# One PSUM tile for the attentions of a restoration block: scores in a ring of seven banks, and half of the keys' 3x3 on VectorE

## The chip, the cores and the metric

The kernel runs on one core of one Trainium2 chip. The metric is the device time of one execution in microseconds. Before the change it is 4100.66 us, the median of three runs (4098.43 to 4103.39). The core has five engines with queues of their own: TensorE (PE, matmuls; PEld are its weight loads), VectorE (DVE), ScalarE (ACT), GpSimd (POOL) and SyncE (SP, which issues the transfers). Matmul results land in PSUM, which has 128 partitions of eight banks, each of 512 float32 values.

## The reference, cut to what matters

The network has four layers, each `x + layer(group_norm(x))`, on an input of 2 images, 128 channels, 64x64 pixels, in float32. Only layer 0 is touched. For each image:

```python
xn = biasfree_ln(gn(x), ln1_w)                    # over the channels
qkv = conv1x1(xn, w_qkv)                          # 128 -> 640 channels
qkv = depthwise_3x3(qkv, w_dw)                    # 640 groups
q1, k1, v, q2, k2 = split(qkv, 5)                 # 128 channels each, 4 heads of 32
q1, k1, q2, k2 = l2 norms over the 4096 tokens of each channel
attn1 = softmax(q1 @ k1.T * temperature)          # 4096 x 4096 per head
out1 = attn1 @ v
attn2 = softmax(q2.T @ k2 * temperature)          # 32 x 32 per head
out = conv1x1(out1 + v @ attn2, w_po)
x = x + conv1x1(biasfree_ln(out, ln2_w), w_proj) + b_proj
```

## The kernel before, in words

Layer 0 is `_layer0`. It goes through the two images in turn: norm, convolutions, attention, finish. The norm of image 1 runs as side work inside the attention of image 0, and the finish of image 0 inside the convolutions of image 1.

**Convolutions** (`convolutions`). The five groups of 128 channels are numbered q1 0, k1 1, v 2, q2 3, k2 4, and each is computed in two halves of 32 image rows, written (group, half). A half first goes through the 1x1 (`pointwise`, L1556): 33 rows (32 and one for the border) in chunks of 16, 16 and 1 rows, into pairs of banks and one single bank, from which ScalarE copies them into a zero-padded frame (L1563). Then comes the 3x3. For q1, k1, q2, k2 it is on TensorE (`depthwise`, L1578): nine taps, each as 16 matmuls of 32x32 diagonal blocks with 512 columns, into two pairs of banks. The banks come out with rows and columns of the head blocks interchanged, and for q1 and k1 eight copies on ScalarE and eight on VectorE (`in_place`, L1598) put the pieces where they belong. For v the 3x3 is on VectorE (`value_taps`, L1614 and L1616): nine operations on 128x2048. Next the squares of each channel are summed (L1603), q1 is scaled by both norms, v is transposed into `vt` (`value_tiles`), and q2 and k2 are transposed and multiplied into one 128x512 accumulator (`products`). All of this is in `_in_order`: each engine keeps the order of the program. The frame for a 3x3 is made two 3x3 ahead.

**Attention** (`attention` with `_attn_four`). There are eight blocks of 512 queries (qb) and 32 tiles of 128 keys (kt), so 256 steps per image. A step computes the scores of the four heads: for each head, whose 32 channels are one row group of TensorE, two matmuls with 64 keys each (L1373), into two pairs of banks. Two Exps of 128x1024 follow on ScalarE (L1382) into a tile `weights` (four buffers). One step later four matmuls (L1790) multiply the weights by `vt` into one accumulator bank. The softmax's denominators: VectorE adds the weights of eight steps (seven adds of 128x2048, L1830) and four matmuls with ones (L1790 too) add that sum to a second accumulator bank. After four such groups, in the fourth step of the next query block, VectorE transposes that bank (L1803), takes the reciprocal, transposes back and multiplies. The order of the instructions here is chosen by a scheduler when the kernel is built; TensorE's is scores of step n+1, then values of step n.

**PSUM.** There are three pairs of banks, `sp()`, taken in turn by the scores, the 1x1, the 3x3 and all side work, and two single banks, `acc(0)` and `acc(1)`.

## Time and profile before

The profiled execution took 4107.57 us; its span from the first to the last instruction is 4105.7 us. Busy times by stage, in us (the span's time, then each engine):

| stage | span | PE | DVE | ACT |
|---|---|---|---|---|
| norm of image 0 | 0 to 37 | 14.7 | 26.6 | 15.8 |
| convolutions, image 0 | 37 to 180 | 131.3 | 74.2 | 64.4 |
| attention, image 0 | 180 to 790 | 599.8 | 541.3 | 513.4 |
| finish of 0 and convolutions, image 1 | 790 to 990 | 176.3 | 113.6 | 77.8 |
| attention, image 1 | 990 to 1590 | 593.5 | 539.2 | 504.5 |
| finish of image 1 | 1590 to 1640 | 38.5 | 38.0 | 6.9 |

The other layers follow until 4105.7. A group's line shows the line of the kernel, the engine, the operation, out<-in with the shapes, the count, busy time and mean ns of one, and the idle time just before with what ended it. The chain of waits lists, in order of time, start, length and what was running or awaited. A timeline gives start, length, engine, line and operation of consecutive instructions, and in brackets the idle time before with its releaser. A float32 matmul leaves two records. Their ends are modelled, so TensorE's busy time includes short waits inside a block.

### The profile page before, as it was taken

To read this page: it belongs to the slowest core of one execution; us is meant where nothing else is said; L and a number is where in the kernel's file an instruction comes from. 1 tells how busy PE (TensorE), PEld (TensorE's weight loads), DVE (VectorE), ACT (ScalarE), POOL (GpSimd) and SP (SyncE) were. 2 spreads that over 40 slices of the span, in tenths; PEclk is the share of its full clock that TensorE was granted. 3 is DMA by queue.
4 is the path that set the end of the run, shared out by engine and by line. 5 is a ranking of instruction groups with operands and counts; after the bars stand their busy time and mean duration, and the time that the engine had idled before them with its cause. 6 is when DMAs were issued, how large, how long until landed. Compare 5 with 4: busy or idle time off the path is not lost.

```text
span 4105.7 us, 83161 instructions
## 1 busy us (share of the span) xinstructions
PE 3941.3 (96%) x35790; PEld 1383.9 (34%) x35790; DVE 3182.5 (78%) x3526; ACT 3231.8 (79%) x3907; POOL 74.2 (2%) x145
## 2 busy tenths in 40 slices
PE   7999999989999998997898999999999999999998
PEld 4522222245222223445666233222322222222222
DVE  4689999846989998986775887777777777776666
ACT  4478888734888884334663899999999999999998
POOL 1001000000000001000000000000000000000000
PEclk9999999999999999998898999999999999999999
DMA  1199960000000000002662211020012101010000
GB/s 50 22 189 189 188 96 2 2 1 2 1 2 2 2 2 13 1 6 111 255 276 105 87 39 32 29 67 27 29 31 61 36 24 32 32 57 6 6 6 4
DMA packets 193134, 217.66 MB, mean 53 GB/s; under 512 B 30442, under 2 KB 154346, under 8 KB 188659
## 3 DMA queue, kind: packets, MB, share of 16 engines
q1 hardware_dynamic: 192754, 212.25, 19.9%
q8 instruction: 282, 4.62, 0.5%
q14 instruction: 98, 0.79, 0.1%
HBM read 178.64 MB, written 98.57 MB: 68 GB/s over the span
## 4 chain that ended last, share of the span: by engine, by line
PE 86%; DVE 8%; ACT 3%; issue 2%; POOL 0%; DMA 0%; SPq 0%; DVEq 0%; POOLq 0%; ACTq 0%
PE ps_acc L2193 24%; PE ps_s L2170 18%; PE ps_s L1373 13%; PE ps_acc L1790 12%; PE ps_sp L1578 4%; PE ps_bank L710 2%; DVE sums L1830 2%; PE ps_z L1008 2%; DVE e L950 1%; PE ps_t L640 1%; PE ps_sp L1556 1%; PE ps_bank L590 1%; PE ps_bank L1062 1%; PE ps_bank L681 1%; ACT weights L1382 1%
## 5 line engine op out<-in xcount | busy, mean ns | idle before, releaser
L2184 ACT ACTIVATE weights<-ps_s 128x1024 f32<-128x1024 f32 x1920 | 1781.8, 1063 | 75.9 <-PE ps_s L2170 75.8
L1382 ACT ACTIVATE weights<-ps_s 128x1024 f32<-128x1024 f32 x1024 | 993.8, 1024 | 168.8 <-PE ps_s L1373 151.1
L2193 PE MATMUL ps_acc<-weights,vt 128*32 128x512 f32 x8192 | 1093.9, 606 | 0.0
L1830 DVE TENSOR_TENSOR sums<-sums,weights 128x2048 f32<-128x2048 f32 x384 | 880.0, 2292 | 45.1 <-ACT weights L1382 8.2
L2170 PE MATMUL ps_s<-q,k 64*128 64x512 f32 x4096 | 830.5, 469 | 3.8 <-DMA k<-stack 2.7
L2170 PEld LDWEIGHTS ps_s<-q,k 64*128 64x128 f32 x4096 | 348.5, 184 | 936.5 <-ACT weights L2184 809.9
L1373 PE MATMUL ps_s<-q,k 32*64 32x512 f32 x8192 | 632.0, 614 | 3.4 <-ACT weights L1382 1.3
L1790 PE MATMUL ps_acc<-weights,vt 128*32 128x512 f32 x4096 | 550.0, 605 | 7.2 <-ACT used L1820 3.7
L2142 DVE SCALAR_TENSOR_TENSOR exp_z<-exp_z,exp_m 128x1024 f32<-128x1024 f32 x384 | 469.2, 1222 | 9.3
L2126 DVE TENSOR_SCALAR exp_i<-ps_s 128x1024 int32<-128x1024 f32 x128 | 156.8, 1225 | 216.8 <-PE ps_s L2170 216.6
L1373 PEld LDWEIGHTS ps_s<-q,k 32*64 32x64 f32 x8192 | 162.1, 130 | 434.8 <-PE ps_s L1373 337.0
L2193 PEld LDWEIGHTS ps_acc<-weights,vt 128*32 128x32 f32 x8192 | 161.9, 108 | 309.8 <-issue 309.0
L1790 PEld LDWEIGHTS ps_acc<-weights,vt 128*32 128x32 f32 x4096 | 81.2, 108 | 427.0 <-issue 403.5
L662 DVE SCALAR_TENSOR_TENSOR X<-g,w,X 128x2048 f32<-128x2048 f32 x84 | 197.4, 2351 | 2.6
L1830 DVE TENSOR_TENSOR sums<-weights 128x2048 f32<-128x2048 f32 x64 | 146.6, 2291 | 61.5 <-ACT weights L1382 61.1
L2146 DVE SCALAR_TENSOR_TENSOR weights<-exp_z,exp_i 128x1024 f32<-128x1024 f32 x128 | 156.8, 1225 | 15.2
L1578 PE MATMUL ps_sp<-pad,diag 32*32 32x512 f32 x4608 | 159.8, 600 | 2.3 <-ACT q L1598 1.3
L2142 DVE SCALAR_TENSOR_TENSOR exp_z<-exp_m 128x1024 f32<-128x1024 f32 x128 | 156.0, 1218 | 0.0
L1008 PE MATMUL ps_z<-w_ri,e 128*32 128x128 f32 x2048 | 137.3, 408 | 14.6 <-DVE e L950 12.3
L1578 PEld LDWEIGHTS ps_sp<-pad,diag 32*32 32x32 f32 x4608 | 96.0, 103 | 54.8 <-issue 17.7
L950 DVE TENSOR_SCALAR e<-ps_pe 32x136 f32<-32x136 f32 (+1 forms) x352 | 104.3, 296 | 4.9
L948 ACT ACTIVATE e<-ps_pe 32x136 f32<-32x136 f32 (+1 forms) x352 | 99.5, 283 | 4.1
(296 smaller groups left out, 2824.7 us busy)
## 6 DMA issues: line engine op xcount, KB each, us to landing
w_ri<-w_r SPq DMA_DIRECT2D x16, 2112.0 KB, 7.9
w_ri<-w_i SPq DMA_DIRECT2D x16, 2112.0 KB, 13.3
stack<-qs SPq DMA_DIRECT2D x64, 256.0 KB, 2.1
q<-stack SPq DMA_DIRECT2D x128, 128.0 KB, 2.5
k<-stack SPq DMA_DIRECT2D x128, 128.0 KB, 2.5
stack<-ks SPq DMA_DIRECT2D x32, 256.0 KB, 2.1
w_r<-in_L_conv_kr_w SPq DMA_DIRECT2D x15, 528.0 KB, 12.8
w_r<-in_L_conv_kr_x SPq DMA_DIRECT2D x15, 528.0 KB, 12.8
```

Of the source, the lines that this page charges most:

```text
L662: nc.vector.scalar_tensor_tensor(xi, g[:, i : i + H // 2, j : j + W], w8[:, s : s + 1], xi, ALU.mult, ALU.add)
L1008: nc.tensor.matmul(out.rearrange("p (n f o) -> p n f o", n=2, f=2), e[:, s, 2 * j : 2 * j + 2, :].rearrange("p f x -> p (f x)"), w.rearran ...
L1373: nc.tensor.matmul(ps[j // 2][to, j % 2, :], k[rows, kt * 128 + 64 * half : kt * 128 + 64 * half + 64], q[rows, qb * CH : (qb + 1) * CH], ...
L1382: nc.scalar.activation(w[:, 2 * p : 2 * p + 2, :], ps[p], AF.Exp)
L1578: nc.tensor.matmul(ps[r // 2][to, r % 2, :].rearrange("p (h w) -> p h w", w=W), diag[rows, grp, t, :], pad[rows, y0 : y0 + ROWS, t % 3 : t ...
L1790: nc.tensor.matmul(ac[n][rows, :], lhs(rows), w[:, j, :], start=first, stop=last)
L1830: nc.vector.tensor_add(parts[0].rearrange("p j c -> p (j c)"), t.rearrange("p j c -> p (j c)"), w.rearrange("p j c -> p (j c)"),)
L2126: nc.vector.tensor_scalar(i, ps.rearrange("p j c -> p (j c)"), EXP_SCALE, EXP_BIAS, ALU.mult, ALU.add)
L2142: nc.vector.scalar_tensor_tensor(z, x, n, m, ALU.add, ALU.mult)
L2170: nc.tensor.matmul(ps[j // 2][:, j % 2, :], g.k[kt // 4][rows, j // 2, keys], g.q[qb][rows, j // 2, :], start=True, stop=True,)
L2184: nc.scalar.activation(w[0], ps[p], AF.Exp)
L2193: nc.tensor.matmul(g.ac[32 * j : 32 * j + 32, :], g.vt[:, kt, j // 2, i : i + 2, :].rearrange("p a d -> p (a d)"), w[:, i, :], start=(at = ...
```

## The change

The change touches layer 0 alone.

- One PSUM tile `banks` of eight banks replaces the two pools. Outside the attention, `sp()` is a pair of its first six banks in turn and `acc(n)` is bank 6 or 7. Inside it, bank 7 is the accumulator of the values and banks 0 to 6 are a ring (`taken()`): a step takes the next four for its scores, and the sums and the side work (`half()`) take one each.
- A step has three Exps instead of two: one bank, two banks, one bank (or one, one, two where the ring wraps).
- The sums no longer have a bank of their own: twice per query block, two groups' sums are added in one bank of the ring by eight matmuls, and VectorE transposes it. The first time it keeps 16 columns (`first`), the second time it adds them and goes on as before. `sums` tiles have three buffers.
- The 3x3 of (1, 0), the first half of the keys, is done by VectorE's taps, as the values are; seven 3x3 on TensorE remain. The taps are spread over the iterations by a new table. The two halves of v are no longer made together: the second half's 1x1 comes two iterations later.
- `pointwise` takes its rows in chunks of 1, 8, 16 and 8, into `acc(0)`, `acc(1)`, a pair, and `acc(0)`.

```diff
+    psp = ctx.enter_context(tc.tile_pool(name="f0_ps", reuse_waits="tile", bufs=1, space=PSUM))
+    banks = psp.tile([128, 8, CH], F32, name="ps")
     def sp():
-        return spp.tile([128, 2, CH], F32, tag="sp", name="ps_sp")
+        n = at["pair"]
+        at["pair"] = (n + 1) % 3
+        return banks[:, 2 * n : 2 * n + 2, :]
     def acc(n):
-        return accp.tile([128, CH], F32, tag=f"acc{n}", name=f"ps_acc{n}")
+        return banks[:, 6 + n, :]
+    def taken():
+        n = at["bank"]
+        at["bank"] = (n + 1) % RING
+        return n
+    def half():
+        return banks[:, taken(), :] if attending[0] else sp()[:, 0, :]
...
-        for r0 in range(0, H // 2 + 1, 2 * ROWS):
-            n = min(2 * ROWS, H // 2 + 1 - r0)
-            ps = sp() if n > 1 else acc(0).rearrange("p (o c) -> p o c", o=1)
+        for r0, n in ((4 * ROWS, 1), (0, ROWS), (ROWS, 2 * ROWS), (3 * ROWS, ROWS)):
+            ps = sp() if n > ROWS else acc(int(r0 == 0)).rearrange("p (o c) -> p o c", o=1)
...
-        order = [(1, 0), (1, 1), (0, 0), (0, 1), (3, 0), (4, 0), (3, 1), (4, 1)]
+        order = [(1, 1), (0, 0), (0, 1), (3, 0), (4, 0), (3, 1), (4, 1)]
+        kpad = frame(pool, "vpad")
+        run(pointwise(kpad, 1, 0))
+        first = taps(1, 0, k1, kpad)
         frames = [frame(pool) for _ in range(2)]
-        for n in range(2):
-            run(pointwise(frames[n], *order[n]))
-        pads = [frame(pool, "vpad") for _ in range(2)]
-        taps = value_taps(pads)
+        run(pointwise(frames[0], *order[0]))
+        next(first)
+        run(pointwise(frames[1], *order[1]))
+        by_vector = first
...
             if n == 0:
-                for half in range(2):
-                    run(pointwise(pads[half], 2, half))
+                by_vector = chain(by_vector, values_of(0))
...
+            if n == 2:
+                squares_of(pool, k1, 0, ss[:, 1, :])
+                by_vector = chain(by_vector, values_of(1))
...
-            for _ in range((0, 0, 3, 3, 4, 4, 4, 0)[n]):
-                next(taps, None)
+            for _ in range(((5, 5, 5, 4, 4, 4, 0), (2, 6, 6, 4, 4, 4, 0))[b > 0][n]):
+                next(by_vector, None)
...
-            while pending:
-                qb, n, w = pending.pop(0)
-                if n == 0:
-                    ac[1] = acc(1)
-                four(1, lambda rows: ones, w, n == 0, n == len(SUMMED) - 1)
-                if n == len(SUMMED) - 1:
+            while len(pending) > 1:
+                (qb, n, one_part), (_, _, other) = pending.pop(0), pending.pop(0)
+                out = banks[:, taken(), :]
+                four(out, lambda rows: ones, one_part, True, False)
+                four(out, lambda rows: ones, other, False, True)
+                by_query = cp.tile([128, CH // 32, 32], F32, tag="g", name="by_query", bufs=1)
+                nc.vector.transpose(by_query.rearrange("p n i -> p (n i)"), out)
+                if n == 0:
+                    firsts[qb] = small.tile([128, CH // 32], F32, tag="first", name="first")
+                    nc.vector.tensor_copy(firsts[qb], by_query[:, :, 0])
+                    continue
...
+                rec = small.tile([128, CH // 32], F32, tag="rec", name="rec")
+                nc.vector.tensor_add(rec, by_query[:, :, 0], firsts.pop(qb))
+                nc.vector.reciprocal(rec, rec)
...
-            if i == 3:
+            if i == 3 and n % 2 == 0:
                 sums()
...
+        def steps():
+            waiting = []
+            for qb in range(NCH):
+                for kt in range(NQT):
+                    at_banks = [taken() for _ in range(4)]
+                    for j in range(4):
+                        rows = slice(32 * j, 32 * j + 32)
+                        for h in range(2):
+                            nc.tensor.matmul(
+                                banks[64 * h : 64 * h + 64, at_banks[j], :],
+                                k1[rows, kt * 128 + 64 * h : kt * 128 + 64 * h + 64],
+                                q1[rows, qb * CH : (qb + 1) * CH],
+                                start=True,
+                                stop=True,
+                            )
+                    w = pool.tile([128, 4, CH], F32, tag="weights", name="weights")
+                    pieces = ((0, 1), (1, 2), (3, 1))
+                    if at_banks[2] < at_banks[1]:
+                        pieces = ((0, 1), (1, 1), (2, 2))
+                    for j, n in pieces:
+                        first = at_banks[j]
+                        nc.scalar.activation(
+                            w[:, j : j + n, :], banks[:, first : first + n, :], AF.Exp
+                        )
...
-        _weave(_attn_four(nc, pool, spp, q1, k1, multiply), side, 4)
+        attending[0] = True
+        _weave(steps(), side, 4)
         sums()
+        attending[0] = False
```

## The prediction

> **What bounds the kernel now.** I read the page's table of engines first, then its costliest groups, then the chain of waits in one quiet stretch of the attention (1400 to 1440 us), the timeline of each engine around one reciprocal of the softmax sums (1515 to 1527 us), and last the chain through batch 0's convolutions (36 to 200 us). The page:
>
> ```profile
> PE 3941.3 (96%) x35790; PEld 1383.9 (34%) x35790; DVE 3182.5 (78%) x3526; ACT 3231.8 (79%) x3907; POOL 74.2 (2%) x145
> ...
> L1382 ACT ACTIVATE weights<-ps_s 128x1024 f32<-128x1024 f32 x1024 | 993.8, 1024 | 168.8 <-PE ps_s L1373 151.1
> L1830 DVE TENSOR_TENSOR sums<-sums,weights 128x2048 f32<-128x2048 f32 x384 | 880.0, 2292 | 45.1 <-ACT weights L1382 8.2
> L1373 PE MATMUL ps_s<-q,k 32*64 32x512 f32 x8192 | 632.0, 614 | 3.4 <-ACT weights L1382 1.3
> ```
>
> TensorE is the bound, and in the two attentions the others follow closely. The chain there, start and length in us:
>
> ```profile
> 1422.78 1.04 PE ps_s L1373 x16
> 1423.82 1.00 PE ps_acc L1790 x8
> 1424.82 1.21 PE ps_s L1373 x16
> 1426.02 1.00 PE ps_acc L1790 x8
> ```
>
> A step is one block of scores and one block of value products. Every second block of scores is 0.17 longer (1.21 against 1.04): its second pair of banks is the pair that the step before used first, and waits for that step's first Exp. Two steps are 4.25 us. Around the reciprocal, VectorE, then TensorE, then ScalarE:
>
> ```profile
> 1515.66 2.29 DVE L1830 TENSOR_TENSOR sums<-weights 128x2048 f32<-128x2048 f32 x1 [1.34 <-ACT weights L1382]
> 1518.06 7.08 DVE L1830 TENSOR_TENSOR sums<-sums,weights 128x2048 f32<-128x2048 f32 x3
> 1525.06 0.71 DVE L1803 STREAM_TRANSPOSE by_query<-ps_acc 128x512 f32<-128x512 f32 x1
> ```
>
> ```profile
> 1519.07 1.11 PE L1373 MATMUL ps_s<-q,k 32*64 32x512 f32 x16
> ...
> 1521.00 1.04 PE L1790 MATMUL ps_acc<-sums,ones 128*32 128x512 f32 x8
> 1521.97 1.11 PE L1373 MATMUL ps_s<-q,k 32*64 32x512 f32 x16
> 1523.02 1.06 PE L1790 MATMUL ps_acc<-weights,vt 128*32 128x512 f32 x8
> 1524.01 1.34 PE L1373 MATMUL ps_s<-q,k 32*64 32x512 f32 x16
> ```
>
> ```profile
> 1520.23 1.94 ACT L1382 ACTIVATE weights<-ps_s 128x1024 f32<-128x1024 f32 x2 [0.26 <-PE ps_s L1373]
> ```
>
> The reader is to see that the transposition ends at 1525.77, which is 1.76 after the second block of scores that follows the sums has begun (1524.01). Today nobody cares, since the sums have a bank of their own. In the convolutions:
>
> ```profile
> 48.79 9.67 PE ps_sp L1578 x263
> ...
> 64.31 3.70 PE ps_sp L1556 x8
> ...
> 71.84 9.66 PE ps_sp L1578 x271
> ...
> 87.43 9.72 PE ps_sp L1578 x268
> ...
> 103.10 9.72 PE ps_sp L1578 x271
> ...
> 118.76 9.75 PE ps_sp L1578 x275
> ```
>
> A 3x3 on TensorE takes 9.7 us; then some 5.9 go by until the next (81.50 to 87.43), while ScalarE's eight copies of 0.58, with a copy of 1.02 between them, and VectorE's eight of 0.69 empty the banks.
>
> **The base.** The profiled execution took 4107.57 us (span 4105.7); the runs' median is 4100.66, 6.9 less. Changes below are differences, added to the median.
>
> **1. Ring and three Exps a step.** The wait of 0.17 goes: a block of scores now takes three free banks and the bank of the step before's first row group, free after a one-bank Exp. No such Exp is in the trace. A ScalarE copy of 128x512 from PSUM takes 0.59 against 1.02 for 128x1024 (L1531, L1563), so 0.425 less; from the Exp's 1.02, and 0.92 from one Exp's start to the next's (1.94 less 1.02), I get 0.60 and 0.495. Scores start to Exp start is 1.16 (1519.07 to 1520.23). So the bank is free at 1.16+0.60 = 1.76, before the next scores want it at 2.04. But what is late next is the value block: it waits for the last Exp. Before, the Exps end 1.16+1.94 = 3.10 after the scores began; now at 1.16+0.495+0.92+0.60 = 3.17, and with 0.05 to be seen 3.22, while TensorE would be there at 2.04+1.04 = 3.08. So 0.14 is lost in every second step where 0.17 was: 0.03 gained a pair, 256 pairs in both attentions, -8 us. Ends: with nothing late, 0.17x256 = -43; with the one-bank Exp like the ScalarE row of 128x512 with a per-partition scale (L1523, 0.69 long, 0.565 apart), the last Exp ends at 3.34 and the pair takes 3.34+0.05+1.00 = 4.39, +36. The plain copy is the nearer row, since Exp and copy of 128x1024 differ by 0.01; I take -8.
>
> The Trainium skill ("ScalarE: Activation LUTs", What ACT_TABLE_LOAD costs) speaks against the split: an ACTIVATE costs 186 ns fixed plus 0.833 ns an element, and back-to-back ones overlap by 93. By it the three end 2.08 after they begin, and a pair would take 4.29, this term +10; by the rows it is -8.
>
> **2. The sums in the ring.** The 16 sum matmuls of a query block stay, but go in two bursts of eight instead of four of four. A burst's bank is the ring's next; the scores behind it take three banks and wrap, and the third row group of the second scores behind it takes the burst's bank. As compiled, that matmul waits for VectorE, and the transposition that frees it stands behind the add of the fifth of eight steps, as it does today. Before, the transposition ends 4.77 after the sums begin (1521.00 to 1525.77) and the second scores begin at 3.01. A burst is one block longer, 0.85 (the chain shows 1.85 for the two together, 1.00 for one), so they begin at 3.86. The wait is 4.77+0.07-3.88 = 0.96 (0.07 for a semaphore, 0.02 for the third row group's place). The adds come every 2.40 against steps of 2.1, and in the new kernel every second burst follows a full reciprocal, so VectorE is some 0.15 later: I take 1.1, range 0.8 to 1.4. All of it is lost: the value block and the next scores stand behind it on TensorE, ScalarE starves behind those. It falls on 15 of 16 bursts a batch (the last is after the loop): 30x1.1 = +33, range 24 to 42. The half reciprocals add to VectorE a transposition (0.75), a copy and an add of 16 columns (0.2 each, from the reciprocal's 0.25) per block: 18 us over 16 blocks. They lie in VectorE's waits at each group's start (1.34, four a block); without that cover, +18.
>
> **3. Keys' first half by VectorE.** Gone from TensorE and ScalarE per batch: one 3x3 (9.7) and its emptying (5.9). VectorE gets 1.28+8x2.39 = 20.4 us, of which it has room: 74 us busy of the 143 in this stage. Batch 0, from the row at 48.79: one more 1x1 (3.7) goes ahead, mostly in TensorE's idle time behind the layer norm, +1.2. The 3x3 that remain are (1,1), (0,0), (0,1) instead of four. Before, their chain runs 48.79 to 118.76. Now: start 50.0, 9.7; then two 1x1 whose first rows wait for the accumulator bank that ScalarE copies last (4.7 of copies of the keys, 0.1+0.47+0.91+0.47 for the frame, then 3.7 for the second 1x1), 10.7; 9.7; 5.8; 9.7; then again two 1x1, the second behind four squares of ScalarE (4x0.96, which wait for VectorE's last copies), 12: 107.6. That is 11 earlier. VectorE is then 2.5 late with its copy of the channel queries and catches up: I take -10. Batch 1: the first 1x1 has no cover (+5.6), the finish of batch 0 stays VectorE's chain, and six taps (14.3) stand before the copies of (0,1), longer than its 3x3 of 9.7, so that squares and the next frame are some 16.4 behind it instead of 5.9. The saved 15.6 is spent: 0. Ends for both: -31 (all of 2x15.6) and +8 (six taps uncovered on top of batch 1).
>
> **4. Rows as 1, 8, 16, 8.** Same five matmuls, a copy more on ScalarE (0.1 apart); counted in 3. The gain is that only one pair of banks is needed, but VectorE's eight copies (5.6) still hold the next 3x3's banks. 0.
>
> **5. Side work in batch 0's attention.** From its first scores to its last it takes 605 us, batch 1's 582; transposes of the norm explain 64x0.15 = 10 of that. The rest, 13, are waits where a side tile takes a pair of three. It now takes a bank of seven. But two transpositions a block share the side's buffer. -4, range -13 to +3.
>
> Sum: -8+33-10-4 = +11: 4112 us.
>
> **The rivals.** (a) *Faster: the convolutions give all back.* If the 1x1's need of one pair frees the 3x3 from its wait, term 3 is -31 instead of -10: 4100.7-8+33-31-4 = 4091. It decides from a saving of 19. For it: 5.9 of waiting behind each of four 3x3. Against: that wait is VectorE's 8x0.69, and VectorE gets more to do. (b) *ScalarE becomes the bound.* Term 1 at +36: 4156. For it: ScalarE has 1.94 of 2.125 busy; against: plain copies are cheap. (c) *The transposition is later, and the convolutions save nothing*: 30x1.4 = +42, -8, 0, 0: 4135. For it: the extra work on VectorE at both places. (d) *The ring doesn't wait* (the change does just what it says): VectorE would have to be 1.1 earlier, and it lags ScalarE by only 0.7 (1522.17 to 1522.85, the fifth step's add), so at least 0.3 stays: 30x0.3 gives 4088.
>
> **How the numbers follow.** Chances: forecast 0.50 (4103 to 4122), (a) 0.14, (d) 0.08, (b) 0.12, (c) 0.16. 0.2% (8 us) is about what can be told from no change; two in five of the forecast lie within it. So slower 0.30+0.12+0.16 = 0.58, faster 0.20, same 0.22. The range 4086 to 4139 takes in (a), (c) and (d), and leaves out (b).
>
> **What would show it.** In the profile after: the score matmuls' weight loads waiting for the transposition, about 1 us, 30 times; ps_s blocks of 1.04 otherwise and value blocks held 0.1 by the last Exp; one-bank Exps of 0.60; first scores of batch 0 some 10 us earlier, of batch 1's convolutions as long as before. Wrong if those waits are absent, if one-bank Exps take 0.69, or if batch 1's convolutions shrink by 10.

## The result, and the profile after

The changed kernel takes 20257.19 us, the median of six runs (20250.71 to 20269.11), against 4099.55 us for the kernel before in the same session (six runs, 4095.76 to 4105.02): 4.941 times as long, 95% interval 4.936 to 4.946. The forecast was 4112. The profiled execution took 20269.11 us, its span is 20267.3.

The page of the changed kernel (engine totals, and some of the costliest groups):

```profile
PE 19695.3 (97%) x79206; PEld 7027.1 (35%) x79206; DVE 8130.3 (40%) x8115; ACT 6902.4 (34%) x8599; POOL 462.8 (2%) x1158
...
L184 DVE TENSOR_REDUCE max_part<-ps_max 128x2 f32<-128x1024 f32 x3072 | 3763.8, 1225 | 7594.2 <-PE ps_max L177 7593.0
...
L226 PE MATMUL ps_s<-q_block,k 128*128 128x512 f32 x12288 | 5890.4, 602 | 19.4 <-POOL q_block L165 19.4
L177 PE MATMUL ps_max<-k,max_block 128*128 128x512 f32 x12288 | 5843.6, 610 | 11.2 <-ACT weights L234 5.9
...
L1884 ACT ACTIVATE weights<-ps 128x512 f32<-128x512 f32 (+1 forms) x1536 | 1027.1, 743 | 150.1 <-PE ps L1871 131.4
L1854 DVE TENSOR_TENSOR sums<-sums,weights 128x2048 f32<-128x2048 f32 x384 | 879.9, 2291 | 47.0 <-ACT weights L1884 15.3
```

The last two lines are layer 0's attention, with the durations forecast: the adds as before, the Exps three a step (their 743 ns are a mean over one-bank and two-bank Exps). The first ones, L177, L184 and L226, are in no page of the kernel before. They belong to code that the change does not touch and that I had left out of my account, the end of the program:

```python
            nc.vector.tensor_scalar(within, top, LIMIT, None, ALU.is_le)
    ok = nc.values_load(within[0:1, 0:1])
    with tc.If(ok == 0):
        _general(tc, a, out)
```

The fast path subtracts no maximum ahead of its Exps. It computes a bound on the scores as it goes (`worst`; for layer 3 from maxima over its queries and keys), and if the bound is over 60, `_general` computes all four layers once more with the maxima. In the changed kernel it does, so the bound has failed: some data of the fast path are wrong. The first pass of the same execution is in the profile too. The last Exp of its layer 0 (image 1) starts at 1594.72 us, in the trace of before at 1582.05: 12.7 later. The time that I forecast is the time of that pass.

What spoiled the data is seen in the finish of image 0, which runs in pieces among image 1's convolutions. It makes `out` of 512 tokens in a PSUM bank (a chunk, L1923), takes its statistics (L1506), and one step later reads the bank again to scale it (`y`, L1515). Between the steps for chunks 5 and 6 the program pauses the finish, and a 3x3 and a 1x1 come in. The timeline of the changed kernel, VectorE, TensorE and ScalarE:

```profile
864.50 0.69 DVE L1515 TENSOR_TENSOR y<-ps,ln_r 128x512 f32<-128x512 f32 x1 [1.19 <-POOL ln_r L1405]
865.76 0.88 DVE L1506 BATCH_NORM_STATS2 ln_st<-ps 128x6 f32<-128x128 f32 x4
...
874.93 3.92 PE L1568 MATMUL ps<-xn,w_qkv 128*128 128x64 f32 x10
...
879.97 1.99 ACT L1575 COPY pad<-ps 128x512 f32<-128x512 f32 x3
...
881.57 0.69 DVE L1515 TENSOR_TENSOR y<-ps,ln_r 128x512 f32<-128x512 f32 x1 [0.84 <-ACT pad L1575]
```

The last line is `y` of chunk 5. It waits for a ScalarE copy of the *1x1* (L1575), where every other `y` waits for its own reciprocal (`ln_r`, as in the first line). It reads a bank that now holds rows of image 1's 1x1. Before, the bank was a tile of a pool, and a tile keeps its buffer until its last reader has been issued; after, `banks` is one tile, `sp()` hands out its pairs in turn, and nothing knows that chunk 5 is still to be read. In the trace of before the `y` on either side of that pause wait for nothing or for `ln_r`:

```profile
866.63 0.69 DVE L1502 TENSOR_TENSOR y<-ps_sp,ln_r 128x512 f32<-128x512 f32 x1
880.64 0.69 DVE L1502 TENSOR_TENSOR y<-ps_sp,ln_r 128x512 f32<-128x512 f32 x1 [1.12 <-POOL ln_r L1404]
```

The attention of the first pass answers to the chain shown of before. Around a reciprocal, the chain of waits of the changed kernel:

```profile
1425.10 2.29 DVE sums L1854
1427.39 0.64 DVE by_query L1822
1428.03 0.04 issue
1428.07 1.09 PE ps L1871 x8
1429.16 1.00 PE ps L1812 x8
1430.15 1.04 PE ps L1871 x16
1431.20 1.00 PE ps L1812 x8
```

The chain leaves TensorE for an add and the transposition (`by_query`), and comes back in the middle of a block of scores: half of its 16 records come after the transposition. This is the wait of term 2, where it was forecast. Away from it, the Exps of the trace mostly begin 2.04 and 2.11 us apart in turn: 4.15 for two steps, against 4.25 before.

### The profile page after: what moved, and what is told of

Same layout as the page of the kernel before. It is cut to its first block, busy times and chain, and to the rows that moved or that the text cites. A ratio compares the mean times of both kernels' runs of the same rounds, so it can differ in the third digit from the quotient of the medians.

```text
span 20267.3 us, 185437 instructions
## 1 busy us (share of the span) xinstructions
PE 19695.3 (97%) x79206; PEld 7027.1 (35%) x79206; DVE 8130.3 (40%) x8115; ACT 6902.4 (34%) x8599; POOL 462.8 (2%) x1158
## 4 chain that ended last, share of the span: by engine, by line
PE 90%; DVE 3%; ACT 1%; issue 0%; DMA 0%; POOL 0%; SPq 0%; ACTq 0%; DVEq 0%; POOLq 0%
PE ps_max L177 28%; PE ps_s L226 27%; PE ps_acc L209 15%; PE ps_acc L2252 5%; PE ps_s L2229 4%; PE ps_acc L313 3%; PE ps L1871 1%; PE ps L1812 1%; PE ps_z L1008 1%; PE ps_bank L710 1%; DVE X L662 1%; DVE r L306 0%; DVE e L950 0%; PE ps_bank L1062 0%; PE ps_bank L590 0%
## 5 line engine op out<-in xcount | busy, mean ns | idle before, releaser
L184 DVE TENSOR_REDUCE max_part<-ps_max 128x2 f32<-128x1024 f32 x3072 | 3763.8, 1225 | 7594.2 <-PE ps_max L177 7593.0
L234 ACT ACTIVATE weights<-ps_s 128x1024 f32<-128x1024 f32 x3072 | 3142.3, 1023 | 10551.8 <-PE ps_s L226 10551.8
L226 PE MATMUL ps_s<-q_block,k 128*128 128x512 f32 x12288 | 5890.4, 602 | 19.4 <-POOL q_block L165 19.4
L177 PE MATMUL ps_max<-k,max_block 128*128 128x512 f32 x12288 | 5843.6, 610 | 11.2 <-ACT weights L234 5.9
L177 PEld LDWEIGHTS ps_max<-k,max_block 128*128 128x128 f32 x12288 | 2164.6, 189 | 3662.0 <-issue 2459.2
L226 PEld LDWEIGHTS ps_s<-q_block,k 128*128 128x128 f32 x12288 | 2254.2, 190 | 3316.3 <-issue 2872.8
L209 PE MATMUL ps_acc<-weights,vt 128*32 128x512 f32 (+1 forms) x12288 | 3259.7, 609 | 1.7 <-ACT weights L234 1.7
L2243 ACT ACTIVATE weights<-ps_s 128x1024 f32<-128x1024 f32 x1920 | 1781.4, 1066 | 76.0 <-PE ps_s L2229 75.8
L1884 ACT ACTIVATE weights<-ps 128x512 f32<-128x512 f32 (+1 forms) x1536 | 1027.1, 743 | 150.1 <-PE ps L1871 131.4
L1871 PE MATMUL ps<-q,k 32*64 32x512 f32 x8192 | 621.7, 615 | 10.0 <-DVE by_query L1822 5.4
L313 PE MATMUL ps_acc<-xn,wc 128*128 128x512 f32 x1440 | 631.2, 594 | 0.0
```

The lines of the kernel that those rows point to most:

```text
L177: nc.tensor.matmul(ps[:, jj, :], qm[:, p + jj, :], k[:, kc * CH : (kc + 1) * CH], start=True, stop=True,)
L184: nc.vector.tensor_reduce(pm[:, p : p + 2, qt, kc], ps, AX.X, ALU.max)
L209: nc.tensor.matmul(acc[0][r : r + hs, :], values(kt, p + jj), w[:, jj, :], start=(kt == 0), stop=(kt == NQT - 1),)
L226: nc.tensor.matmul(ps[:, jj, :], k[:, kt * 128 : (kt + 1) * 128], qm[:, p + jj, :], start=True, stop=True,)
L234: nc.scalar.activation(w, ps, AF.Exp)
L313: nc.tensor.matmul(out, wc[:, t, grp * C : (grp + 1) * C], xn[:, c * ROWS + t // 3 : (c + 1) * ROWS + t // 3, t % 3 : t % 3 + W], start=(t ...
```

## The experiments

There are three questions: what makes the second computation run, what the first pass's terms are worth, and whether a version without the fault gains. The kernel with only the fault mended is called the mended kernel below.

### What makes the second computation run

Two theories: (A) chunk 5's bank is handed on in the pause; (B) two score matmuls that the scheduler has put among image 0's convolutions (at 143.97 us, 47 us ahead of the others) spoil a bank there. The first run mends A alone:

```diff
-            if 1 <= c < NCH + 1:
+            if 1 <= c < NCH + 1 and c - 1 not in y:
                 y[c - 1] = scaled(ps[c - 1], r[c - 1])
...
                 r[c] = spread(ps[c])
+                if c == 5:
+                    y[c] = scaled(ps[c], r[c])
```

> The changed kernel, but the finish of image 0 makes y of chunk 5 from its PSUM bank in the step that filled it, ahead of the pause of the finish, and not in the next step behind the pause. Theory A (bank handed on): in the pause the 1x1 of the next frame writes into that bank, chunk 5 of image 0 becomes wrong, the bound on the scores fails and the whole network is computed a second time. Then this kernel takes 4112 us (4099.6 + the 12.2 by which the changed kernel's layer 0 ends later, in its trace 1592.2 against 1580.0), range 4104 to 4120, and none of the general path's lines are in its profile. Theory B (scores too early): the two score matmuls at 143.97 us, among image 0's convolutions, spoil a bank; then it stays at 20257.

Measured: 4110.23 us against 4101.1 (ratio 1.0023, 1.0014 to 1.0032), with 82582 instructions instead of 185437, none on L177, L184 or L226. The second run mends B alone:

```diff
-            attention(pool, chain(*side))
+            with _behind_pe(tc):
+                attention(pool, chain(*side))
```

`_behind_pe` makes every matmul of the attention depend on the last one ahead of it.

> The changed kernel with one thing more: every matmul of an attention is kept behind the last matmul of the convolutions ahead of it, so that no score matmul comes among them. Theory B (scores too early spoil a bank): 4112 us. Theory A (the bank of chunk 5 is handed on in the pause of the finish): the second computation stays, 20257 us within 15.

Measured: 20258.57 us (one run); its first scores now start at 192.75 us, behind the convolutions, and the second computation runs all the same. B has fallen and A stands. Third, the kernel before with a bound that always fails:

```diff
-LIMIT = 60.0
+LIMIT = 0.0
```

> The kernel before with the bound set to 0 instead of 60, so that its test always fails and the general path runs behind the fast one. By theory A the changed kernel's time is its own fast path and this second computation, 20257.2 less 4111.8 = 16145 us; the kernel before should then take 4099.6 + 16145 = 20245 us, within 15. If the changed kernel's fast path were itself slow, this would be shorter by as much.

Measured: 20247.46 us (one run), 2 from the forecast. Its page has the same group at the same cost:

```profile
L226 PE MATMUL ps_s<-q_block,k 128*128 128x512 f32 x12288 | 5889.3, 602 | 18.5 <-POOL q_block L165 18.5
```

So 16147 of the 16158 us are the second computation (20257.19 less 4110.23), and the kernel before has it in store too. Last, the changed kernel without the branch:

```diff
-    ok = nc.values_load(within[0:1, 0:1])
-    with tc.If(ok == 0):
-        _general(tc, a, out)
```

> The changed kernel without the branch that computes the network a second time; the second computation is left out, and chunk 5 of image 0 stays wrong by theory A. Both theories: 4112 us, range 4104 to 4120. Over 4125 would say that the first pass has lost time at a place that neither names.

Measured: 4101.59 us (1.0004 of before, 0.9994 to 1.0015), 8.6 below the mended kernel. Its layer 0 is not shorter: from first to last Exp 1400.2 us (194.11 to 1594.28), mended 1398.8. In these two traces the difference lies behind layer 0, and includes the branch itself: the first of the output's last four transfers is issued 7.4 us ahead of the end of the span in the mended kernel, 4.3 without the branch. The rest isn't shown to be the branch's: from the start of layer 0's last Exp to the end of the span pass 2521.6 us in the mended kernel and 2513.5 without the branch, but also 2510.4 and 2524.7 in two kernels below (the ring of six, and the rows of before), which have the branch and the same code there.

### What the terms of the first pass are worth

By stage, in us, from the starts of the Exps of the profiled executions ("between" runs from the last Exp of image 0 to the first of image 1; a quiet query block is one without side work; the mended kernel is the one that makes `y` of chunk 5 early):

| kernel | first Exp | attention 0 | between | attention 1 | a quiet query block | median | to before |
|---|---|---|---|---|---|---|---|
| before | 193.6 | 603.4 | 204.2 | 580.8 | 71.80 | 4101.1 | 1 |
| changed, first pass | 194.6 | 610.2 | 198.0 | 591.9 | 72.70 | | |
| mended | 191.4 | 610.8 | 194.5 | 593.5 | 72.70 | 4110.2 | 1.0023 |
| with the rows of before | 193.9 | 609.7 | 194.6 | 593.7 | 72.70 | 4112.8 | 1.0039 |
| with the convolutions of before | 201.5 | 611.2 | 203.3 | 594.9 | 72.70 | 4130.4 | 1.0082 |
| ring of six | 190.5 | 638.1 | 199.8 | 618.1 | 76.6 | 4165.5 | 1.0170 |
| ring that passes over a bank | 189.1 | 606.3 | 198.0 | 584.0 | 71.60 | 4100.4 | 1.0009 |
| and two Exps behind a burst | 190.1 | 601.8 | 194.1 | 578.7 | 70.72 | 4088.0 | 0.9973 |
| and sums added in turn | 189.1 | 596.1 | 192.1 | 576.7 | 70.72 | 4072.4 | 0.9937 |

The kernel before had medians of 4101.1, 4095.8 and 4098.5 us in the sessions of these runs, so kernels of different sessions are compared by their ratios to it below (0.001 is 4.1 us). Changed and mended differ by 3.2 in the first column, where their code is the same, and the kernel before has 200.1 in the third column in its trace with the bound at 0. So a stage of one trace carries 3 to 4 us of scatter.

The convolutions first. One run takes back the rows alone:

```diff
-        for r0, n in ((4 * ROWS, 1), (0, ROWS), (ROWS, 2 * ROWS), (3 * ROWS, ROWS)):
-            ps = sp() if n > ROWS else acc(int(r0 == 0)).rearrange("p (o c) -> p o c", o=1)
+        for r0 in range(0, H // 2 + 1, 2 * ROWS):
+            n = min(2 * ROWS, H // 2 + 1 - r0)
+            ps = sp() if n > 1 else acc(0).rearrange("p (o c) -> p o c", o=1)
```

> The kernel that makes chunk 5 early (4110.2 us), with the 1x1's rows in chunks of 16, 16 and 1 as before, the keys' first half still by VectorE. Theory C (the rows cost): in the changed kernel TensorE stands idle for 3.16 us ahead of the 1x1 at 70.16 us and again ahead of the one at 109.38, because the first chunk takes the bank that ScalarE copies last; then its granted clock is 0.5 to 0.64 and the two 1x1 take 7.0 and 5.8 us instead of 3.7. With the rows of before the idle time is about 1.5, the clock stays at 1.0, and 4 to 9 us of image 0 and as much of image 1 at most are saved: 4104 us, range 4094 to 4108. By my prediction (rows change nothing): 4110.

Measured: 4112.79 us (1.0039 of before, 1.0024 to 1.0055): no gain, rather a loss of 0.0016, 7 us, with intervals that overlap. Theory C fails with it. Between the first two 3x3 of image 0 the idle times become 0.47 and 2.28 us, and TensorE's clock falls all the same (0.52, the third figure from the end, in the stretch from 64 to 68 us):

```profile
64.62 8.11 PE L1569 MATMUL ps<-xn,w_qkv 128*128 128x512 f32 x14 [2.28 <-ACT k L1611]
```

```profile
64.00:68.00 4.00, 3.38 (x6) 1.83 (x7) 3.93 (x3) 1.83 (x4) 0.00 (x0) 0.52 0.00 0
```

Another run takes back the rows and the whole of `convolutions`, so that the ring and the single tile remain:

```diff
-        order = [(1, 1), (0, 0), (0, 1), (3, 0), (4, 0), (3, 1), (4, 1)]
+        order = [(1, 0), (1, 1), (0, 0), (0, 1), (3, 0), (4, 0), (3, 1), (4, 1)]
...
-            for _ in range(((5, 5, 5, 4, 4, 4, 0), (2, 6, 6, 4, 4, 4, 0))[b > 0][n]):
-                next(by_vector, None)
+            for _ in range((0, 0, 3, 3, 4, 4, 4, 0)[n]):
+                next(taps, None)
...
```

> The kernel that makes chunk 5 early, with the convolutions as they were: rows of 16, 16 and 1, and eight 3x3 on TensorE; the ring and its sums stay. By my prediction the keys' taps and the rows are worth 10 us: 4120. By the traces of before and after, image 0's convolutions end 1.0 later with the change and image 1's take 198.0 instead of 204.2 us from the last Exp to the first: they are worth 5, and this takes 4115, range 4110 to 4121.

Measured: 4130.38 us (1.0082, 1.0068 to 1.0096). Keys' taps and rows together are worth 0.0059, 24 us, of which some 7 are the rows', by a difference that isn't clear of the noise. The same convolutions end 7.9 later in image 0 than in the kernel before (201.5 against 193.6), and the reason is the tile. TensorE's timeline, first before, then here, between two 3x3:

```profile
100.62 1.99 PE L1556 MATMUL ps_sp<-xn,w_qkv 128*128 128x512 f32 x4 [1.51 <-ACT pad L1563]
```

```profile
100.43 1.13 PE L1569 MATMUL ps<-xn,w_qkv 128*128 128x512 f32 x2 [0.47 <-ACT q L1611]
103.85 1.29 PE L1569 MATMUL ps<-xn,w_qkv 128*128 128x512 f32 x4 [2.29 <-ACT q L1611]
```

Before, the second 16 rows wait for the copy of the first 16 (`pad`): the pool gave them that pair again. With pairs in turn they get a pair that the 3x3 has just filled, and wait for the copies that empty it (`q`), 2.76 instead of 1.51 us in all. So the 3x3 with one 1x1 between them start 16.8 us apart instead of 15.7, three times in image 0. The last 3x3 of image 0, which waits for copies of the value tiles (1.85 us, 0.34 before), takes 13.6 us from the start of its first matmul to that of its last, instead of 10.5; some 1.6 of that are the clock, which falls behind the wait: the 284 records after it take 11.33 us, before 9.72.

Now the ring. Two runs take the wait for the transposition away, in two manners. In the first the ring has six banks and the sums one of their own, in four bursts, as before:

```diff
-RING = 7
+RING = 6
...
-                out = banks[:, taken(), :]
-                four(out, lambda rows: ones, one_part, True, False)
-                four(out, lambda rows: ones, other, False, True)
+                if n == 0:
+                    summed[0] = acc(0)
+                four(summed[0], lambda rows: ones, w, n == 0, n == len(SUMMED) - 1)
...
-            if i == 3 and n % 2 == 0:
+            if i == 3:
                 sums()
```

> The kernel that makes chunk 5 early, with a ring of six banks, and bank 6 for the sums alone: four bursts of four matmuls and one transposition per query block, as before the change; three Exps a step stay. By my prediction's terms 1 and 2 the wait of some 1.1 us for the transposition, twice per query block, costs 33; and steps of 2.04 and 2.11 in turn (4.15 a pair) need no seventh bank, since the fourth row group's bank is free 2.7 us after the scores before it began and is wanted at 2.8. So a query block takes 70.2 instead of 72.7 us and this kernel 4110.2 - 40 = 4070, range 4062 to 4085. The rival, that ScalarE or VectorE takes up the wait: over 4090.

Measured: 4165.51 us (1.017, 1.0153 to 1.0186), 60 *slower* than the mended kernel by the ratios. TensorE's timeline:

```profile
1450.40 1.35 PE L1867 MATMUL ps<-q,k 32*64 32x512 f32 x16
...
1452.68 1.48 PE L1867 MATMUL ps<-q,k 32*64 32x512 f32 x16
```

Most blocks of scores take 1.29 to 1.78 us (these 1.35 and 1.48), where one that finds its banks free takes 1.11. I had supposed that the four row groups of a block start one after the other, 0.26 apart. In the trace eight matmuls, two of each row group, start within 0.05 us of each other; the fourth row group wants its bank at once, and it is freed last. With seven banks only one bank of the step before is needed, the first one freed: that is what the seventh bank is for. The second manner leaves the ring and passes over the sums' bank once:

```diff
         n = at["bank"]
         at["bank"] = (n + 1) % RING
+        if n in held:
+            held.remove(n)
+            return taken()
         return n
...
-                out = banks[:, taken(), :]
+                bank = taken()
+                held.append(bank)
+                out = banks[:, bank, :]
...
-                    pieces = ((0, 1), (1, 2), (3, 1))
-                    if at_banks[2] < at_banks[1]:
-                        pieces = ((0, 1), (1, 1), (2, 2))
+                    pieces = [(0, 1), (1, 1), (2, 1), (3, 1)]
+                    for j in (1, 2, 0):
+                        if at_banks[j] + 1 == at_banks[j + 1]:
+                            pieces[j : j + 2] = [(j, 2)]
+                            break
```

The last piece keeps three Exps a step: the two-bank Exp takes two banks that still lie side by side.

> The kernel that makes chunk 5 early, with a ring of seven that passes over the bank of a burst of sums once, the next time it comes round, so that no score waits for the transposition; everything else stays. TensorE could then do a query block in 70.2 us, VectorE's work per block is 28 adds of 2.39, three transpositions of 0.75 and some 1.5 of small work, 70.7. So 72.7 becomes about 70.8: 4110.2 - 30 = 4080, range 4070 to 4092. If the wait is only moved (VectorE as late, ScalarE starved): 4105 to 4112.

Measured: 4100.43 us (1.0009, 1.0000 to 1.0017): 6 of the 30 us by the ratios, 10 by the medians. The next run is built on the reading of the six banks, that the wait left is for the second Exp of the step behind the burst:

```diff
+                behind[0] = True
...
+                    if behind[0]:
+                        for j in (2, 0):
+                            if at_banks[j] + 1 == at_banks[j + 1]:
+                                pieces[j : j + 2] = [(j, 2)]
+                        behind[0] = False
+                    else:
...
```

> The ring that passes over the sums' bank (4100.4 us), and the step right behind a burst has two Exps of two banks instead of three. Theory D (row groups side by side): the scores' four row groups start within 0.03 us of each other, so in the step where the ring passes over a bank, the fourth row group at once wants the bank that is freed by the second Exp of the step before; that is the 0.64 by which the second step behind a burst still takes 2.71 instead of 2.07 us. With a first Exp of two banks both are free at 1.16+1.02 = 2.18 us behind the start of the scores, against 2.04 when they are wanted: the step takes 2.2. That is 0.5 for 30 bursts: 4100.4 - 15 = 4085, range 4080 to 4093. If VectorE (70.7 of work in a query block of 71.6) holds it instead: 4093 to 4102.

Measured: 4088.03 us (0.9973, 0.9963 to 0.9983). The second block of scores behind a burst in TensorE's timelines, in the mended kernel, with the bank passed over (at most bursts; at others it takes 1.35), and with two Exps:

```profile
1458.86 2.19 PE L1871 MATMUL ps<-q,k 32*64 32x512 f32 x16
```

```profile
1483.88 1.78 PE L1877 MATMUL ps<-q,k 32*64 32x512 f32 x16
```

```profile
1472.40 1.34 PE L1879 MATMUL ps<-q,k 32*64 32x512 f32 x16
```

Of 1.08 above a plain 1.11, first 0.67 and then 0.23 are left. Theory D stands, and the time is the one forecast from it (4085, range 4080 to 4093). Last, VectorE:

```diff
-            n, i = places[kt]
-            if i == 3 and n % 2 == 0:
+            i = kt % 16
+            p = i // 4 if i < 6 else i % 2
+            if i == 3:
                 sums()
-            if i == 0:
-                parts[0] = w
+            if i in (0, 4):
+                parts[p] = w
...
```

> The same with the sums of two groups added in turn: within 16 steps the even and the odd ones from the sixth on go to two tiles in turn, so that an add follows one of the other tile. In the trace of before, adds that follow on themselves start 2.39 us apart and independent ones 2.21: 10 of 14 adds save 0.18, 3.6 us of VectorE a query block. If VectorE sets the pace of the ring that passes over a bank, a query block falls to TensorE's 70.2: 4078, range 4070 to 4085. If not, it is as without: within 4 us of the kernel that has the two Exps alone.

Measured: 4072.40 us (0.9937, 0.9924 to 0.9950), the best of all, 0.6% below the kernel before. The gain is not where I expected it: a quiet query block takes 70.72 as without, so TensorE was its bound already. The ten adds in a row of VectorE's timeline are nevertheless 2.20 apart,

```profile
1429.95 22.10 DVE L1863 TENSOR_TENSOR sums<-sums,weights 128x2048 f32<-128x2048 f32 x10
```

and the attentions are 5.7 and 2.0 us shorter, in the query blocks that carry side work. VectorE has more to do there, which is the likely reason; no run tests it. That is 8 of the 11 us by which the two traces differ (15 by the ratios); the other 3 lie in the first and third column, within the scatter of one trace.

### The idle time that slows TensorE's clock

In the first pass of the changed kernel a 1x1 takes 3.92 us, but the second of two in a row 7.00 and 5.81. TensorE's timeline, and stretches of 4 us (length; busy time of PE, PEld, DVE, ACT, POOL with counts; granted clock; DMA share, GB/s):

```profile
63.08 3.92 PE L1568 MATMUL ps<-xn,w_qkv 128*128 128x64 f32 x10
70.16 7.00 PE L1568 MATMUL ps<-xn,w_qkv 128*128 128x64 f32 x10 [3.16 <-ACT pad L1575]
77.09 9.79 PE L1590 MATMUL ps<-pad,diag 32*32 32x512 f32 x288
...
109.38 5.81 PE L1568 MATMUL ps<-xn,w_qkv 128*128 128x64 f32 x10 [3.16 <-ACT pad L1575]
```

```profile
64.00:68.00 4.00, 3.00 (x7) 0.97 (x6) 3.91 (x6) 3.88 (x8) 0.13 (x1) 1.00 0.00 0
68.00:72.00 4.00, 1.84 (x4) 1.26 (x5) 3.92 (x4) 3.94 (x7) 0.00 (x0) 0.70 0.01 2
72.00:76.00 4.00, 4.00 (x6) 1.48 (x5) 3.96 (x2) 1.02 (x4) 0.00 (x0) 0.50 0.00 0
```

TensorE waits 3.16 us for ScalarE to free the single bank that the first chunk wants; then its clock is 0.50, where behind the 1.5 us of idle time of the kernel before it stayed at 1.00. The Trainium skill ("TensorE: Matmul & The Clock Gate", Part 1) gives half rate after an idle window of about 3.4 us, and full rate after a busy one; the 0.50 agrees; by the modelled ends, 3.16 us were enough here. The length of one idle time doesn't settle it, though: in the kernel before, the clock stayed at 1.00 behind 3.08 us without a matmul as well (147.56 to 150.64). Two runs tried to win it back. The first emits the values' 1x1 ahead of the squares and takes the 16 rows first:

```diff
-        for r0, n in ((4 * ROWS, 1), (0, ROWS), (ROWS, 2 * ROWS), (3 * ROWS, ROWS)):
-            ps = sp() if n > ROWS else acc(int(r0 == 0)).rearrange("p (o c) -> p o c", o=1)
+        for r0, n in ((0, 2 * ROWS), (4 * ROWS, 1), (2 * ROWS, ROWS), (3 * ROWS, ROWS)):
+            ps = sp() if n > ROWS else acc(int(r0 == 2 * ROWS)).rearrange("p (o c) -> p o c", o=1)
...
+                if n in (0, 2):
+                    by_vector = chain(by_vector, values_of(n // 2))
                 squares_of(pool, out, half, ss[:, grp, :])
...
-                by_vector = chain(by_vector, values_of(0))
...
-                by_vector = chain(by_vector, values_of(1))
```

> The kernel that makes chunk 5 early (4110.2 us), with the values' 1x1 emitted ahead of the squares of the 3x3 before it, and the rows in chunks of 16, 1, 8, 8, the 16 into a pair first. Theory C (the second 1x1 costs): between the first two 3x3 of image 0 lie 14.2 us, between the third and fourth 13.3, since the second 1x1 stands idle for 3.16 us for the bank that ScalarE copies last, the granted clock then falls to 0.5 and its copies stand behind squares. Now the first chunk needs only a pair that is emptied at about 68.1 instead of 70.2, the clock stays at 1.0, and no square is ahead: 1.7 and 2 to 3.5 us of image 0 and as much of image 1, 4102, range 4097 to 4107. If the 3x3 wait for VectorE's copies anyway, or the norms become late: 4108 to 4114.

Measured: 4121.56 us (1.0059, 1.0046 to 1.0072), 15 slower by the ratios than the mended kernel. The last chunk now waits for the bank of the single row, whose copy stands behind eight of the keys':

```profile
67.36 6.75 PE L1568 MATMUL ps<-xn,w_qkv 128*128 128x512 f32 x12 [3.05 <-ACT pad L1575]
```

The idle time is 3.05 instead of 3.16, only elsewhere. The second, on the best kernel, keeps the rows in the changed kernel's order, emits the values' 1x1 early too, and fills the gap with a matmul whose result nobody reads:

```diff
             pad = frame(pool, "vpad")
+            nc.tensor.matmul(acc(1), w_qkv[:, :C], xn[:, :CH], start=True, stop=True)
             run(pointwise(pad, 2, half))
...
+                if n in (0, 2):
+                    by_vector = chain(by_vector, values_of(n // 2))
                 squares_of(pool, out, half, ss[:, grp, :])
...
-                by_vector = chain(by_vector, values_of(0))
...
-                by_vector = chain(by_vector, values_of(1))
```

> The ring that passes over a bank, two Exps behind a burst, and sums added in turn (4072.4 us), with two things more: one matmul of 512 columns without use into the idle single bank ahead of the values' 1x1, and the values' 1x1 emitted ahead of the squares, the rows in the changed kernel's order of 1, 8, 16, 8. Theory C once more: the idle 3.16 us ahead of the second 1x1 are what halves TensorE's clock, and squares on ScalarE hold its last chunk (6.4 us of idle time in image 1, 893.9 to 900.4). With the matmul between, no idle time there is over 2 us, the clock stays at 1.0 there, and the second 1x1 of image 0 take some 4 instead of 5.6 and 5.8 us: 3 us in image 0 and 5 to 7 in image 1, 4063, range 4058 to 4069. If it is VectorE's copies and taps that hold the 3x3, or the clock falls anyway: 4069 to 4078.

Measured: 4077.57 us (0.9953, 0.9940 to 0.9967), 5 to 7 above the kernel without (0.9937, 0.9924 to 0.9950), with intervals that overlap; its first Exp comes at 196.7 us instead of 189.1. TensorE's timeline and stretches:

```profile
66.48 1.12 PE L1697 MATMUL ps<-xn,w_qkv 128*128 128x512 f32 x2 [1.75 <-ACT pad L1580]
67.89 5.52 PE L1573 MATMUL ps<-xn,w_qkv 128*128 128x64 f32 x10 [0.28 <-ACT pad L1580]
...
104.22 1.12 PE L1697 MATMUL ps<-xn,w_qkv 128*128 128x512 f32 x2 [1.75 <-ACT pad L1580]
105.62 3.92 PE L1573 MATMUL ps<-xn,w_qkv 128*128 128x64 f32 x10 [0.28 <-ACT pad L1580]
...
129.21 1.17 PE L1595 MATMUL ps<-pad,diag 32*32 32x512 f32 x16 [5.15 <-DVE qk L1606]
```

```profile
68.00:72.00 4.00, 4.00 (x8) 1.97 (x9) 3.93 (x3) 0.80 (x2) 0.00 (x0) 0.61 0.00 0
...
104.00:108.00 4.00, 3.50 (x9) 1.58 (x10) 1.19 (x2) 2.37 (x5) 0.00 (x0) 1.00 0.00 0
```

At the second place (104 us) the clock stays at 1.00 and the 1x1 takes 3.92 us; in the best kernel without the extra matmul the same 1x1 takes 5.81. So the slow clock is what these 1.9 us cost. At the first place (66 us) the idle times are the same, 1.75 and 0.28 us, and the clock falls all the same: that 1x1 takes 5.52. What decides between the two places no run shows. Then, four records into the next 3x3, TensorE waits 5.15 us for VectorE's copy of the channel queries (`qk`), where the best kernel has no such wait. VectorE's timeline says why, first in the best kernel, then here:

```profile
106.17 0.16 DVE L1502 TENSOR_REDUCE nq<-ss 128x1 f32<-128x4 f32 x1 [2.59 <-ACT junk L1620]
...
109.69 11.89 DVE L1632 SCALAR_TENSOR_TENSOR v<-vpad,wd,v 128x2048 f32<-128x2048 f32 x5
121.61 1.23 DVE L1606 COPY qk<-ps 128x1024 f32<-128x1024 f32 x1
```

```profile
112.49 0.16 DVE L1502 TENSOR_REDUCE nq<-ss 128x1 f32<-128x4 f32 x1 [7.28 <-ACT junk L1620]
...
116.01 11.89 DVE L1632 SCALAR_TENSOR_TENSOR v<-vpad,wd,v 128x2048 f32<-128x2048 f32 x5
127.93 1.23 DVE L1606 COPY qk<-ps 128x1024 f32<-128x1024 f32 x1
```

VectorE sums up the squares (`junk`) for the norm of q1, and five taps and the copy stand behind that in its order. ScalarE makes the squares behind the copies of the values' 1x1 now, so VectorE waits 7.28 us for them instead of 2.59, and the copy comes 6.3 us later. In the run before, VectorE waits 10.03 us at this place, and TensorE 4.63 for `qk`. So by the traces the loss comes from the new place of the values' 1x1; the extra matmul alone, with the 1x1 where it was, remains untested.

## Why the prediction was wrong

**The step that failed is the base.** "Changes below are differences, added to the median" takes for granted that everything outside the five terms stays as it is, and the end of the program does not: it branches on the data. The term that is missing is +16147, the second computation. The change says that pool tiles become slices of one tile; I costed that as banks and waits (term 5: "It now takes a bank of seven") and did not ask which slices are still to be read when the next is handed out. The finish of image 0 stood in the prediction only as "VectorE's chain". No rival was "it computes something else", though the diff shows a pool's protection being removed, and that is the rival that happened.

**The sum for the first pass held, by luck.** Forecast +11, measured +9.1 with the fault mended (4110.23 against 4101.1; 6 to 13 by the interval). By its terms:

- *Term 2* (the transposition, 30 x 1.1 = +33): right. In a quiet query block two steps take 3.12 and 3.27 instead of 2.04, together 2.31; times 15, for 15 of each 16 bursts, 34.6. The runs that pass over the bank and then free two together bring a block from 72.70 to 71.60 and 70.72.
- *Term 1* (-8): the mechanism was right, its size too small. A block is 0.90 longer in all, so the rest of it gains 1.41, 22.6 over 16 blocks. About 0.4 of that are two bursts (1.72 and 1.78 over a plain step) in place of four (1.02, three times, and 0.86), which I took as equal; 1.0 is the pair of steps: 4.15 instead of 4.25, where my sum had 4.22 (4.29 by the skill's figures). The value blocks are held less by the last Exp than the 0.14 of my estimate: they take 1.13 or 1.14 at such steps, 1.07 at others. One-bank Exps take 0.60, as estimated.
- *Term 3* (-10 in image 0, 0 in image 1): the taps, with the rows, are worth what I said in image 0 (201.5 to 194.6 and 191.4: 7 and 10), and 5 and 9 in image 1, where I had nothing. What is missing is the price of the tile, 7.9 in image 0: the pairs in fixed turn. Against the kernel before, image 0's first Exp comes 1.0 later in the changed kernel, 2.2 earlier in the mended one.
- *Term 4* (0): right within the noise (7 us in favour of the new rows, with intervals that overlap), but not for my reason. In the run with the rows of before, the second 16 rows wait 0.47 and 2.28 us for the pair that a 3x3 has filled, with the new ones the first chunk waits 3.16 for a single bank, and the clock falls behind both.
- *Term 5* (-4): about 0. What the first three query blocks of image 0 take above quiet ones was 30.1 (83.1+87.7+74.7 less three of 71.8) and is 29.3 in the changed kernel; in image 1 it grew from 7.2 to 11.0.

So +11 would have become +11 + 8 (tile) - 15 (term 1) - 7 (term 3, image 1) + 7 (term 5) + 2 (term 2) + 1.5 (term 3, image 0) = +7.5, each stage with its 3 to 4 us of scatter. That the sum held is luck: errors of 8, 15 and twice 7 us cancelled. The rivals (a) to (d) were all about the first pass; (d), a ring that does not wait, was had only by changing it.

## What to carry to other kernels

Where a change turns pool tiles into slices of one tile, list every slice that is read after another may be handed out, above all across a pause of a generator: the pool was what kept them apart. Where a program ends in a branch on its own results, put that branch into the forecast, as a rival with its own price. And a ring is only as good as the order in which its banks come free: passing over one bank and freeing two together at one step was worth 20 us, while a ring with a bank less, and that bank kept for the sums, was 60 slower, although it did away with the same wait.

## What the runs showed of the hardware

- 32-row matmuls on four row groups start side by side, eight within 0.05 us: a block wants all its banks at once, so one late bank delays the block (1.29 to 1.78 us instead of 1.11 in the ring of six, 2.19 behind a burst).
- Behind 3.16 us without a matmul TensorE's granted clock was 0.50 for several microseconds, and a 1x1 took 5.81 or 7.00 us instead of 3.92. But the length of one idle time does not decide alone: behind 1.75 us the clock was 1.00 at one place and fell at another of the same trace, and behind 3.08 us it stayed at 1.00 in the kernel before.
- VectorE adds of 128x2048 that follow on an independent one start 2.20 us apart instead of 2.39, in ten adds in a row.
- The test at the end of the program costs time even when it passes: some 3 us behind the last output by two traces (7.4 against 4.3). Without it the changed kernel takes 8.6 us less than the mended one by the medians; no run shows that the rest is the test's.
